# Unmasked attention by sorting and prefix sums instead of a full aggregation, in a four-layer graph attention kernel

## The chip, the cores and the metric

The kernel runs on one core of a Trainium2 chip. The metric is the device time of one execution in microseconds (us). Engines: TensorE (PE; its weight loads are PEld), VectorE (DVE), ScalarE (ACT), GpSimd (POOL) and SyncE (SP), which issues most DMAs. Each engine works through its own queue in order; semaphores tie the queues together.

## The reference

`x` has shape (32, 512, 256): 32 independent batches of 512 tokens with 256 features. Four layers follow each other, and all of them add to `x`. Each starts with a layer norm and a ReLU, and holds one or two graph attentions. An attention computes `h = inp @ W`, a score per pair of tokens from two numbers per token, and a softmax-weighted mean of the rows of `h`:

```python
def _gat(inp, adj_mask, W, a):
    h = jnp.matmul(inp, W)
    f1 = jnp.matmul(h, a[:F_, 0]); f2 = jnp.matmul(h, a[F_:, 0])
    e = jax.nn.leaky_relu(f1[:, :, None] + f2[:, None, :], ALPHA)
    if adj_mask is not None:
        e = jnp.where(adj_mask[None, :, :] > 0, e, NEG_INF)
    att = jax.nn.softmax(e, axis=2)
    h_prime = jnp.einsum('bij,bjf->bif', att, h)
    return jax.nn.elu(h_prime)
# layer 3
out = relu(x @ mlp1_w + mlp1_b);  residual = out            # 256 -> 512
out = elu(_gat(relu(out), None, W_fc, a_fc)) + residual     # no mask, 512 wide
out = relu(out @ mlp2_w + mlp2_b); residual = out           # 512 -> 256
out = relu(elu(_gat(relu(out), adj, W_hand, a_hand)) + residual)
```

Layers 0 and 1 have one masked attention of 256 features, layer 2 has four masked heads of 64, and layer 3 is the block above. Its first attention has no mask: every token sees all 512.

## The kernel before

All arithmetic is in float32. The 512 tokens are four tiles of 128 partitions (`NT = 4`). The attention weight exp(leaky_relu(r + t)) is written, after common factors are taken out, as the larger of a number of the row (`r`) and a number of the column (`t`), times a factor of the column that is multiplied into the values. So `weights` (L238 to L252) transposes `r` into a bank of PSUM by four TensorE transposes (L243), and VectorE takes the maximum with `t` and multiplies by the mask (L247; without a mask L251). `aggregate` (L257, matmuls at L259) multiplies the 512 x 512 weights with the values; a column of factors beside the values gives the denominator (L263 takes its reciprocal). The unmasked attention of layer 3 does this with 512 columns of values in two halves: 257 and 256 columns, four output tiles, four matmuls each.

The norm (`norm_t`, L177 on) takes statistics on VectorE (L182, L183), the reciprocal root on POOL (L185, L186), and writes `xn` on VectorE (L190). `xn` is transposed (L198), and ScalarE evicts it with the ReLU (L199). `linear_t` (L234, evicted at L235) and the value matmuls (L216, L317, L357) follow. `elu2_plus1` (L284 to L287) applies two ELUs with a min on VectorE, an Exp on ScalarE and an add on POOL.

Batches run in four streams (`NS = 4`); stream i takes batches i, i+4 and so on. Each layer is a Python generator that yields between steps, and a loop takes one step of each stream in turn:

```python
while live:
    for g in list(live):
        if next(g, live) is live:
            live.remove(g)
```

Before the next stream joins, the ones that are there take 20 rounds (`LEAD`). The order in which instructions are written is their priority; the scheduler of the framework, which simulates the engines, then fixes each engine's order when the kernel is built. Tiles come from pools with a number of buffers for each tag: eight banks of PSUM (`b`) for all streams, five weight tiles `w` of 8 KB a partition, three `v`, two `v2` and `v3`, eight `y`.

At the end the kernel computes a flag from the mask and from the largest exponential it has seen (`seen`, L208). If it is set, a general version of the kernel runs instead. With the given inputs it does not.

Of the kernel before, what the change touches and what calls it, by code (L numbers as in the profile page):

```python
# [21 lines left out]
I32 = mybir.dt.int32  # L22
AF = mybir.ActivationFunctionType
# [6 lines left out]
NEG = -(2.0 ** 100)  # L30


@with_exitstack
def fast(ctx, tc, flag, x, adj, w0, a0, w1, a1, w2, a2, mlp1_w, mlp1_b, mlp2_w, mlp2_b,
# [10 lines left out]
    LEAD = 20  # L45
# [3 lines left out]
    psum = ctx.enter_context(tc.tile_pool(name="psum", bufs=1, space=bass.MemoryType.PSUM))  # L49

    def bank():
        return psum.tile([P, N], FP, tag="b", name="b", bufs=8)
# [9 lines left out]
    def load_x(b):  # L62
        t = work.tile([P, NT, F], FP, tag="x", name="x", bufs=NS + 1)
        nc.sync.dma_start(t, x[b].rearrange("(t p) f -> p t f", p=P))
        return t
# [16 lines left out]
    def project(dst, block, kt, a_cols):  # L82

        ft, n = a_cols.shape[1], a_cols.shape[2]
        for k in range(kt):
            p = bank()
            for f in range(ft):
                nc.tensor.transpose(p[:, f * P:(f + 1) * P], block(k, f), ident)
            wT = work.tile([P, N], FP, tag="y", name="wT", bufs=8)
            nc.scalar.copy(wT[:, :ft * P], p[:, :ft * P])  # L90
            q = bank()
            for f in range(ft):
                nc.tensor.matmul(
                    q[:, :n], wT[:, f * P:(f + 1) * P], a_cols[:, f, :], start=(f == 0), stop=(f == ft - 1)
                )
# [22 lines left out]
    adj_sb = work.tile([P, NT, N], I32, tag="w", name="adj", bufs=5)  # L118
    nc.sync.dma_start(adj_sb, adj.rearrange("(t p) j -> p t j", p=P))
    pos = work.tile([P, NT, N], FP, tag="w", name="pos", bufs=5)  # L120
    nc.vector.tensor_scalar(pos, adj_sb, 0.0, None, op0=OP.is_gt)
    own = work.tile([P, NT, N], FP, tag="w", name="own", bufs=5)
# [5 lines left out]
    for j in range(NT):  # L128
        p = bank()
        for t in range(NT):  # L130
            nc.tensor.transpose(p[:, t * P:(t + 1) * P], own[:, t, j * P:(j + 1) * P], ident)
# [8 lines left out]

    W1 = load_w(w1, a1, 0.01, "W1")
    CH = D + 3
    W2 = const.tile([P, KF, NH, CH], FP, name="W2")
    raw2 = work.tile([P, KF, F], FP, tag="y2", name="raw2", bufs=4)
# [32 lines left out]
    def norm_t(xt):  # L177
# [9 lines left out]
        yield  # L187
        xn = work.tile([P, NT, F], FP, tag="xn", name="xn", bufs=3)
        for t in range(NT):
            nc.vector.tensor_scalar(  # L190
                xn[:, t, :], xt[:, t, :], mv[:, t, 0:1], rs[:, t:t + 1], op0=OP.subtract, op1=OP.mult
            )
        yield
        hT = work.tile([P, KF, N], FP, tag="hT", name="hT", bufs=3)
        for k in range(KF):
            p = bank()
            for t in range(NT):
                nc.tensor.transpose(p[:, t * P:(t + 1) * P], xn[:, t, k * P:(k + 1) * P], ident)  # L198
            nc.scalar.activation(hT[:, k, :], p, AF.Relu)  # L199
        yield  # L200
# [9 lines left out]
    def values(hT, w):  # L210

        v = work.tile([P, NT, F + 3], FP, tag="v", name="v", bufs=3)
        for t in range(NT):
            ps = bank()
            for k in range(KF):
                nc.tensor.matmul(  # L216
# [5 lines left out]
            if t % 2:  # L222
                yield
# [3 lines left out]
    def linear_t(inT, w, bias, name):  # L227
# [3 lines left out]
        for f in range(ft):  # L231
            p = bank()
            for k in range(kt):
                nc.tensor.matmul(p, w[:, k, f * P:(f + 1) * P], inT[:, k, :], start=(k == 0), stop=(k == kt - 1))  # L234
            nc.scalar.activation(o[:, f, :], p, AF.Relu, bias=bias[:, f:f + 1])  # L235
            yield
        return o

    def weights(r_col, t_col, masked=True):

        r = bank()
        for t in range(NT):
            nc.tensor.transpose(r[:, t * P:(t + 1) * P], r_col(t).to_broadcast([P, P]), ident)  # L243
        wt = work.tile([P, NT, N], FP, tag="w", name="w", bufs=5)
# [9 lines left out]
    def pair():  # L254
        return work.tile([P, 2, F], FP, tag="y", name="y", bufs=8)

    def aggregate(p, wt, t, rhs):  # L257
        for j in range(NT):
            nc.tensor.matmul(p, wt[:, j, t * P:(t + 1) * P], rhs(j), start=(j == 0), stop=(j == NT - 1))  # L259
# [6 lines left out]
    def plain(hT, w):  # L266
        v = yield from values(hT, w)
        wt = weights(lambda t: v[:, t, F + 2:F + 3], lambda j: v[:, j, F + 1:F + 2])
        yield
# [19 lines left out]
    def layer0(xt):  # L289
        v, wt = yield from plain((yield from norm_t(xt)), W0)  # L290
        for t0 in range(0, NT, 2):
            r, q = pair(), pair()
            for i in range(2):
                p, rd = averages(v, wt, t0 + i)
                nc.scalar.activation(q[:, i, :], p, AF.Exp, scale=rd)  # L295
                nc.scalar.activation(r[:, i, :], p, AF.Relu, scale=rd)
            add_elu(xt[:, t0:t0 + 2, :], r, q)
            yield

    def layer1(xt):  # L300
        v, wt = yield from plain((yield from norm_t(xt)), W1)
        for t0 in range(0, NT, 2):
            r = pair()
            for i in range(2):
                p, rd = averages(v, wt, t0 + i)
                nc.scalar.activation(r[:, i, :], p, AF.Relu, scale=rd)
            xr = xt[:, t0:t0 + 2, :]
            nc.gpsimd.tensor_tensor(xr, xr, r, op=OP.add)  # L308
            yield

    def layer2(xt):
        hT = yield from norm_t(xt)
        v = work.tile([P, NT, NH, CH], FP, tag="v2", name="v2", bufs=2)
        for t in range(NT):
            ps = bank()
            for k in range(KF):
                nc.tensor.matmul(  # L317
# [7 lines left out]
            if t % 2:  # L325
                yield
        note(v.rearrange("p t h c -> p (t h) c")[:, :, D:])
        ys = [pair(), pair()]
        for h in range(NH):
            wt = weights(lambda t: v[:, t, h, D + 2:D + 3], lambda j: v[:, j, h, D + 1:D + 2])  # L330
            yield
# [5 lines left out]
            for i in range(2):  # L337
# [548 lines left out]
```

## Time and profile before

| | |
|---|---|
| median of 3 runs | 3417.73 us (3411.73 to 3418.64) |
| profiled execution, its own time | 3417.93 us |
| its span, first to last instruction | 3416.2 us |
| granted TensorE clock, mean | 0.977 |
| busy: PE, PEld, DVE, ACT, POOL | 3314.6, 2750.0, 1700.9, 1380.6, 571.7 us |
| HBM read, written | 20.99, 16.78 MB |

A row of a group of instructions reads: line, engine, operation, output <- inputs, shapes, count, then busy time in us and mean ns of one, then the idle time of the engine just before them and what ended it. A float32 matmul leaves two records in the trace, a transpose one. Matmuls overlap at their ends, so the busy times of groups add up to more than the engine's busy time. In the waits, the first name is who waited and the second is what came last. The granted clock is the share of full speed that TensorE was given.

### The profile page before, as it was taken

The numbers are of one execution on the slowest core, as the hardware profiler recorded it, in microseconds if no ns is written. First come the engines' busy times: TensorE is split into PE (matmuls) and PEld (weight loads), VectorE is DVE, ScalarE is ACT, GpSimd is POOL, SyncE is SP. The second block draws the span as 40 slices with busy tenths as digits, with TensorE's granted clock in tenths as the row PEclk, the third lists the DMA queues.
The fourth block names the chain that finished last, engine by engine and source line by source line (L and its number), as shares of the span: only waits on it lengthen the run. The fifth ranks groups of instructions, "written<-read, shape, count | busy, mean of one in ns | idle before, by whom it ended". The sixth has DMA issues, their size and how long they took to land.

```text
span 3416.2 us, 44221 instructions
## 1 busy us (share of the span) xinstructions
PE 3314.6 (97%) x17265; PEld 2750.0 (80%) x17265; DVE 1700.9 (50%) x4422; ACT 1380.6 (40%) x3281; POOL 571.7 (17%) x583
## 2 busy tenths in 40 slices
PE   6899999999999999999999999999999999999997
PEld 5688888788887887878878888788888788887875
DVE  3554563554644655446544455454653545635542
ACT  2234434444334434344334443444434444344433
POOL 0111111211112111121111121112201111112111
PEclk8899999999999999999999999999999999999999
DMA  2000000000000000000000000000000000000000
GB/s 80 1 1 13 13 1 13 13 13 13 1 13 13 13 13 1 13 19 7 13 13 1 25 7 7 13 1 25 13 1 13 11 16 13 1 13 7 7 7 14
DMA packets 41606, 40.67 MB, mean 12 GB/s; under 512 B 5296, under 2 KB 40624, under 8 KB 41392
## 3 DMA queue, kind: packets, MB, share of 16 engines
q1 hardware_dynamic: 41392, 37.77, 3.6%
q8 instruction: 140, 2.29, 0.3%
q14 instruction: 74, 0.61, 0.1%
HBM read 20.99 MB, written 16.78 MB: 11 GB/s over the span
## 4 chain that ended last, share of the span: by engine, by line
PE 87%; DVE 6%; ACT 3%; POOL 3%; issue 1%; DMA 0%; SPq 0%; POOLq 0%; ACTq 0%; DVEq 0%
PE b L259 43%; PE b L357 13%; PE b L234 11%; PE b L216 8%; PE b L317 3%; PE b L198 3%; PE b L243 3%; PE b L387 1%; DVE xn L190 1%; POOL y L287 1%; DVE st L182 1%; DVE x L281 1%; POOL rs L186 1%; PE b L405 1%; DVE y L280 1%
## 5 line engine op out<-in xcount | busy, mean ns | idle before, releaser
L259 PE MATMUL b<-v,w 128*128 128x257 f32 (+2 forms) x9216 | 1657.9, 337 | 19.2 <-DVE w L247 16.9
L259 PEld LDWEIGHTS b<-v,w 128*128 128x128 f32 x9216 | 1457.2, 194 | 218.5 <-issue 44.0
L247 DVE SCALAR_TENSOR_TENSOR w<-b,v,maskT 128x512 f32<-128x512 f32 x896 | 609.2, 744 | 37.3 <-PE b L243 37.3
L287 POOL TENSOR_TENSOR y<-y 128x512 f32<-128x512 f32 x192 | 243.4, 1268 | 1799.2 <-ACT y L286 1566.7
L263 DVE RECIPROCAL rden<-b 128x1 f32<-128x1 f32 (+1 forms) x640 | 101.9, 166 | 756.2 <-PE b L259 755.4
L357 PE MATMUL b<-WFC,oT 128*128 128x259 f32 (+1 forms) x2048 | 466.4, 380 | 0.0
L357 PEld LDWEIGHTS b<-WFC,oT 128*128 128x128 f32 x2048 | 381.9, 189 | 62.5 <-issue 8.1
L190 DVE TENSOR_SCALAR xn<-x,mv,rs 128x256 f32<-128x256 f32 x512 | 190.8, 432 | 153.1 <-POOL rs L186 153.1
L216 PE MATMUL b<-W,hT 128*128 128x259 f32 x1024 | 263.4, 402 | 2.1 <-ACT hT L199 2.0
L182 DVE BATCH_NORM_STATS2 st<-x 128x6 f32<-128x256 f32 x512 | 194.4, 406 | 98.3 <-POOL x L308 67.1
L234 PE MATMUL b<-hT,WM 128*128 128x512 f32 x512 | 240.8, 593 | 0.0
L234 PE MATMUL b<-oT,WM 128*128 128x512 f32 x512 | 232.2, 596 | 0.5 <-DVE oT L390 0.5
L216 PEld LDWEIGHTS b<-W,hT 128*128 128x128 f32 x1024 | 195.4, 200 | 34.2 <-ACT hT L199 7.3
L295 ACT ACTIVATE y<-b,rden 128x256 f32<-128x256 f32 x128 | 60.8, 475 | 395.6 <-DVE rden L263 395.6
L379 ACT ACTIVATE y<-b,rden 128x256 f32<-128x256 f32 x256 | 123.2, 481 | 222.7 <-DVE rden L263 173.1
L199 ACT ACTIVATE hT<-b 128x512 f32<-128x512 f32 x256 | 142.3, 595 | 143.7 <-PE b L198 142.5
L221 ACT ACTIVATE v<-b,v 128x256 f32<-128x256 f32 x384 | 182.5, 475 | 12.5
L234 PEld LDWEIGHTS b<-oT,WM 128*128 128x128 f32 x512 | 95.8, 191 | 95.4 <-issue 87.5
L285 DVE TENSOR_SCALAR y<-y 128x512 f32<-128x512 f32 x192 | 82.4, 429 | 178.5 <-ACT y L379 142.4
L364 ACT ACTIVATE v<-b,v 128x256 f32<-128x256 f32 x256 | 121.5, 475 | 117.8 <-PE b L357 113.6
L198 PE MATMUL b<-ident,xn 128*128 128x128 f32 x1024 | 145.0, 283 | 19.1 <-DVE xn L190 19.1
L286 ACT ACTIVATE y<-y,minus 128x512 f32<-128x512 f32 x192 | 138.8, 723 | 57.3 <-DVE y L285 41.4
(99 smaller groups left out, 2892.8 us busy)
## 6 DMA issues: line engine op xcount, KB each, us to landing
x<-in_x_dram SPq DMA_DIRECT2D x32, 512.0 KB, 3.8
out_dram<-x SPq DMA_DIRECT2D x32, 512.0 KB, 2.9
adj<-in_adj_dram SPq DMA_DIRECT2D x1, 1024.0 KB, 8.1
WM<-in_L_gnn_mlp_w_dram SPq DMA_DIRECT2D x2, 512.0 KB, 5.4
WFC<-in_L_gnn_W_fc_dram SPq DMA_DIRECT2D x2, 512.0 KB, 5.7
W<-in_L_gnn_W_dram SPq DMA_DIRECT2D x2, 256.0 KB, 7.8
raw<-in_L_gnn_W_dram SPq DMA_DIRECT2D x1, 256.0 KB, 5.6
WHA<-in_L_gnn_W_hand_dram SPq DMA_DIRECT2D x1, 256.0 KB, 6.2
```

The lines of the kernel that those rows point to most:

```text
L182: nc.vector.bn_stats(st[:, t, :], xt[:, t, :])
L190: nc.vector.tensor_scalar(xn[:, t, :], xt[:, t, :], mv[:, t, 0:1], rs[:, t:t + 1], op0=OP.subtract, op1=OP.mult)
L198: nc.tensor.transpose(p[:, t * P:(t + 1) * P], xn[:, t, k * P:(k + 1) * P], ident)
L199: nc.scalar.activation(hT[:, k, :], p, AF.Relu)
L216: nc.tensor.matmul(ps[:, :F + 3], hT[:, k, t * P:(t + 1) * P], w[:, k, :], start=(k == 0), stop=(k == KF - 1))
L221: nc.scalar.activation(v[:, t, :F], ps[:, :F], AF.Copy, scale=pj)
L234: nc.tensor.matmul(p, w[:, k, f * P:(f + 1) * P], inT[:, k, :], start=(k == 0), stop=(k == kt - 1))
L247: nc.vector.scalar_tensor_tensor(wt[:, j, :], r, t_col(j), maskT[:, j, :], op0=OP.max, op1=OP.mult)
L259: nc.tensor.matmul(p, wt[:, j, t * P:(t + 1) * P], rhs(j), start=(j == 0), stop=(j == NT - 1))
L286: nc.scalar.activation(q, q, AF.Exp, bias=minus1)
L287: nc.gpsimd.tensor_tensor(r, r, q, op=OP.add)
L357: nc.tensor.matmul(ps[c][:, :n], oT[:, k, t * P:(t + 1) * P], WFC[:, k, c * (F + 3):c * (F + 3) + n], start=(k == 0), stop=(k == KH - 1),)
```

## The change

1. **The unmasked attention.** For a row with number r, the tokens with t below r contribute r times their value, and the others t times their value. With the tokens sorted by t, the sum of any row is therefore r times a prefix sum of the values plus a suffix sum of t times the values, both read at the place where r falls. The changed kernel no longer builds the 512 x 512 weights there. It transposes `t` (`tj`), finds each token's rank by comparing with all others on VectorE (ties broken by the token's index, `tie`), and finds the place of each r by a sum of signs on ScalarE. Four indirect DMAs from POOL scatter the rows of `v3` to DRAM (`order`) in sorted order. SP reads them back in two halves of 258 columns, four consecutive sorted rows a partition. POOL and VectorE add the four rows up inside the partition, two matmuls with triangular matrices (`before`, `after`) carry the sums across partitions, and SP writes the 513 rows of prefix and suffix sums to DRAM (`table`). Four indirect DMAs gather one row of the table for each token, and VectorE, ScalarE and POOL finish as before.
2. **The norm.** `xn` is written by ScalarE, with scale and bias and the ReLU, from two more small POOL operations. The eviction of the transposes is a plain copy.
3. **Streams.** Each stream has a clock; the stream with the earliest clock takes the next step. The clock advances by the time of the step's TensorE columns times 2.4 and by the number that the step yields. Streams start 80 apart.
4. **Buffers.** Every stream has two PSUM banks and one `x` tile of its own. `w` has four buffers, `v` and `v2` share four, `v3` has one, `y` and `q` three each; layer 2 writes one tile `y4`.

The core of the diff (`matmul` and `transpose` count columns and call TensorE):

```diff
     def bank():
-        return psum.tile([P, N], FP, tag="b", name="b", bufs=8)
+        return psum.tile([P, N], FP, tag=f"b{turn[0]}", name="b", bufs=8 // NS)
...
+        mr = small([NT], "mr")
+        nc.gpsimd.tensor_tensor(mr, mv[:, :, 0], rs, op=OP.mult)
+        nc.gpsimd.tensor_scalar_mul(mr, mr, -1.0)
+        yield 4
+        xn = work.tile([P, NT, F], FP, tag="xn", name="xn", bufs=2)
         for t in range(NT):
-            nc.vector.tensor_scalar(
-                xn[:, t, :], xt[:, t, :], mv[:, t, 0:1], rs[:, t:t + 1], op0=OP.subtract, op1=OP.mult
-            )
+            nc.scalar.activation(xn[:, t, :], xt[:, t, :], AF.Relu, bias=mr[:, t:t + 1], scale=rs[:, t:t + 1])
...
         note(v[:, :, F:F + 3])
-        wt = weights(lambda t: v[:, t, F + 2:F + 3], lambda j: v[:, j, F + 1:F + 2], masked=False)
-        yield
-        for t in range(NT):
-            y, q = pair(), pair()
-            for c, n in ((0, F + 1), (1, F)):
-                ps = bank()
-                aggregate(ps[:, :n], wt, t, lambda j: v[:, j, c * (F + 3):c * (F + 3) + n])
-                if c == 0:
-                    rd = reciprocal(ps[:, F:F + 1])
-                nc.scalar.activation(q[:, c, :], ps[:, :F], AF.Exp, scale=rd)
-                nc.scalar.activation(y[:, c, :], ps[:, :F], AF.Relu, scale=rd)
-            elu2_plus1(y, q)
+        tj = work.tile([P, N], FP, tag="tj", name="tj", bufs=1)
+        p = bank()
+        for t in range(NT):
+            transpose(p[:, t * P:(t + 1) * P], v[:, t, F + 1:F + 2].to_broadcast([P, P]), ident)
+        nc.scalar.copy(tj, p)
+        yield 1
+        found = small([2, NT], "found")
+        for t in range(NT):
+            nc.vector.scalar_tensor_tensor(
+                junk, tj, v[:, t, F + 1:F + 2], tie(t), op0=OP.subtract, op1=OP.is_lt,
+                accum_out=found[:, 0, t:t + 1],
+            )
+            nc.scalar.activation(
+                junk, tj, AF.Sign, bias=v[:, t, F + 2:F + 3], scale=-1.0, accum_out=found[:, 1, t:t + 1]
+            )
+        at = work.tile([P, 2, NT], U32, tag="at", name="at", bufs=4)
...
+        order = dram.tile([N, H + 3], FP, tag="order", name="order", bufs=2)
+        for t in range(NT):
+            nc.gpsimd.indirect_dma_start(
+                out=order, out_offset=bass.IndirectOffsetOnAxis(ap=at[:, 0, t:t + 1], axis=0),
+                in_=v[:, t, :], in_offset=None,
+            )
+        yield 18
+        for c in range(2):
+            flat = work.tile([P, NT * 2, C], FP, tag="sums", name="sums", bufs=2)
+            sums = flat.rearrange("p (t k) n -> p t k n", k=2)
+            u = sums[:, :, 1, :]
+            nc.sync.dma_start(u, rows[:, :, c * (F + 1):c * (F + 1) + C])
...
+            nc.gpsimd.tensor_tensor(sums[:, 2, 0, :], u[:, 0, :], u[:, 1, :], op=OP.add)
+            nc.gpsimd.tensor_tensor(sums[:, 3, 0, :], sums[:, 2, 0, :], u[:, 2, :], op=OP.add)
+            nc.gpsimd.tensor_tensor(tot, sums[:, 3, 0, :], u[:, 3, :], op=OP.add)
+            nc.vector.tensor_scalar_mul(u[:, 3, :], u[:, 3, :], T[:, 3:4])
+            for t in (2, 1, 0):
+                nc.vector.scalar_tensor_tensor(
+                    u[:, t, :], u[:, t, :], T[:, t:t + 1], u[:, t + 1, :], op0=OP.mult, op1=OP.add
+                )
+            yield 5
+            pv, pu = bank(), bank()
+            matmul(pv[:, :C], before, tot, start=True, stop=True)
+            matmul(pu[:, :C], after, u[:, 0, :], start=True, stop=True)
+            nc.scalar.copy(sums[:, 0, 0, :], pv[:, :C])
+            nc.vector.tensor_tensor(
+                sums[:, 1:, 0, :], sums[:, 1:, 0, :], pv[:, None, :C].to_broadcast([P, NT - 1, C]), op=OP.add
+            )
+            nc.vector.tensor_tensor(u, u, pu[:, None, :C].to_broadcast([P, NT, C]), op=OP.add)
...
+            nc.sync.dma_start(places[:, :, c, :], flat)
+            nc.sync.dma_start(table[N:, c * C:(c + 1) * C], tot[P - 1:, :])
+            yield 10 * c
+        for t in range(NT):
+            y, q = pair(), pair("q")
+            g = work.tile([P, 4 * C], FP, tag="g", name="g", bufs=3)
+            nc.gpsimd.indirect_dma_start(
+                out=g, out_offset=None, in_=table,
+                in_offset=bass.IndirectOffsetOnAxis(ap=at[:, 1, t:t + 1], axis=0),
+            )
+            z = g[:, :2 * C]
+            nc.vector.scalar_tensor_tensor(z, z, rr[:, t:t + 1], g[:, 2 * C:], op0=OP.mult, op1=OP.add)
+            rd = reciprocal(z[:, F:F + 1])
+            nc.scalar.activation(q, z, AF.Exp, scale=rd)
+            nc.scalar.activation(y, z, AF.Relu, scale=rd)
+            elu2_plus1(y, q)
+            yield 6
+            p = bank()
+            for f in range(KH):
+                transpose(p[:, f * P:(f + 1) * P], y.rearrange("p a f -> p (a f)")[:, f * P:(f + 1) * P], ident)
...
+    live = {i: i * LEAD for i in range(NS)}
+    streams = [stream(i) for i in range(NS)]
     while live:
-        for g in list(live):
-            if next(g, live) is live:
-                live.remove(g)
+        i = min(live, key=live.get)
+        turn[0], spent[0] = i, 0.0
+        wait = next(streams[i], None)
+        if wait is None:
+            del live[i]
+        else:
+            live[i] += STRETCH * spent[0] / CYCLES + wait
```

## The prediction

> **What bounds the kernel now.** I read the page's busy times first, then busy time by windows, the chain of waits, the groups with shapes kept apart, and the DMA issues. From the page (busy us, share of the span, instructions; the chain by engine):
>
> ```profile
> PE 3314.6 (97%) x17265; PEld 2750.0 (80%) x17265; DVE 1700.9 (50%) x4422; ACT 1380.6 (40%) x3281; POOL 571.7 (17%) x583
> ...
> PE 87%; DVE 6%; ACT 3%; POOL 3%; issue 1%; DMA 0%; SPq 0%; POOLq 0%; ACTq 0%; DVEq 0%
> ```
>
> TensorE sets the end; nobody else is above 50%. The windows (busy time of PE, PEld, DVE, ACT, POOL, then the granted clock) show that this holds all through:
>
> ```profile
> 440.88:853.94 413.06, 408.33 (x2145) 339.81 (x2145) 210.94 (x549) 170.98 (x408) 71.14 (x72) 0.99 0.03 11
> ```
>
> 413.06 us is one round of four batches, 103.3 a batch, and PE idles 1% of it. What the change takes off PE therefore comes off the end one for one, until a new wait fills the hole. The outer stretches are different:
>
> ```profile
> 120.00:130.00 10.00, 10.00 (x39) 8.48 (x39) 4.04 (x10) 1.68 (x4) 0.00 (x0) 0.75 0.00 0
> 130.00:140.00 10.00, 5.16 (x38) 4.52 (x37) 7.02 (x22) 3.76 (x8) 1.26 (x2) 0.77 0.01 2
> 3300.00:3320.00 20.00, 18.71 (x124) 15.33 (x122) 10.01 (x22) 5.38 (x11) 2.53 (x2) 1.00 0.01 1
> ```
>
> Near the start, where PE has idled, the granted clock is 0.75 even in a window that is 100% busy: 2.5 us of 10 are lost. A PE gap can cost more than its own length.
>
> **PE work removed and added.** The chain in order of time gives PE time without overlaps (start, us, what):
>
> ```profile
> 3363.15 14.13 PE b L259 x64
> ```
>
> These 64 records (a float32 matmul leaves two) are the unmasked aggregation of one batch: 32 matmuls, 0.442 us each. All 32 batches: 452.2 us, gone. Added are four 128x258 triangular matmuls a batch, 128 in all, at the same 0.442: 56.6. The transposes keep their number (four for `tj` instead of four for `r`; 16 of `y`). Net -395.6 us, 12.4 a batch. PE's steady need is then 91 us a batch.
>
> **The other engines.** By the groups (busy, mean ns):
>
> ```profile
> L190 DVE TENSOR_SCALAR xn<-x,mv,rs 128x256 f32<-128x256 f32 x512 | 190.8, 432 | 153.1 <-POOL rs L186 153.1
> L221 ACT ACTIVATE v<-b,v 128x256 f32<-128x256 f32 x384 | 182.5, 475 | 12.5
> L186 POOL TENSOR_TENSOR rs<-rs,neg_half 128x4 f32<-128x4 f32 x128 | 135.0, 1060 | 6.7
> L251 DVE TENSOR_SCALAR w<-b,v 128x512 f32<-128x512 f32 x128 | 90.9, 746 | 17.3 <-PE b L243 17.3
> L287 POOL TENSOR_TENSOR y<-y 128x512 f32<-128x512 f32 x192 | 243.4, 1268 | 1799.2 <-ACT y L286 1566.7
> ```
>
> DVE loses the norm's 190.8, the 90.9 of L251 and 8 in layer 2. It gains 128 searches like L247 (0.744): 95; 256 products of 258 columns at L190's 0.432: 111; per half a 774-, a 1032- and a small 258-column add from PSUM, at L390's 684 ns for 512 scaled up about 0.95 + 1.22 + 0.42, times 64: 166; 128 combinations at L280's 0.70: 90; small copies 26. DVE: about 1900 us. ACT gains 512 norms at L221's 0.475 (243), 128 Signs at 0.72 (92), copies (80), and saves 85 where 512 reads of a half row become 256 of a whole row: about 1710. POOL gains 256 four-element operations at L185's 0.226 (58) and 192 adds of 258 columns (1.268 x 258/512 = 0.64: 123), and the making of 256 indirect DMAs: bounds per issue are 0.23 (L185) and 1.06 (L186, whose ucode also loops), I take the middle 0.64: 164. About 920. Against a span near 3200 these are 59%, 53% and 29%: covered by PE, at no cost, as long as no PE instruction waits for their queues. If that cover went, DVE's extra 200 us is the most it could show.
>
> **The new waits, which decide.** Layer 3 now leaves the chip twice. Engines run their queues in order, so the question is how much PE work the built order puts between the steps. I priced the changed kernel's PE order with the rows above (group sums scaled by 0.927, since the groups of before add up to 3575 us against 3314.6 busy). The same four distances repeat each round, one per stream:
> - last `tj` transpose to first `before` matmul: 21.6, 24.8, 21.8, 23.6; mean 22.9 us
> - last `after` matmul to the first `y` transpose: 16.3, 17.2, 16.3, 11.3; mean 15.3 us
>
> Against the first stands: copy of `tj` 0.60 (L199); the stretch of DVE's queue from the first search to the index copy, 5.3 to 7.3, mean 6.2; four scatters, each waiting for the landing of the one before (all write `order`), 4S; the read of half the rows, 516 KB; three POOL adds 1.9. DMA rows (KB each, us to landing):
>
> ```profile
> x<-in_x_dram SPq DMA_DIRECT2D x32, 512.0 KB, 3.8
> out_dram<-x SPq DMA_DIRECT2D x32, 512.0 KB, 2.9
> adj<-in_adj_dram SPq DMA_DIRECT2D x1, 1024.0 KB, 8.1
> A<-in_L_gnn_a_dram SPq DMA_DIRECT2D x8, 0.2 KB, 2.5
> ```
>
> The read is 3.8, so the need is 12.5 + 4S. The trace has no DMA from POOL and none that is indirect. S is bounded by 2.5, the quickest landing, and 8.1, the slowest; a gain is excluded, the old kernel had no such step. The nearest row is the 2.9 store; with 0.64 to make it, S = 3.5. Need 26.5 against 22.9: PE waits 3.6 us a batch.
>
> The Trainium skill, DMA: Bandwidth & Descriptors, section Anatomy of one DMA, fits a POOL-issued DMA as 2.0 us plus bytes/436e3: 2.6 us for a scatter of 258 KB, as an estimate. No run here shows it yet; by it the first wait would vanish and the end would be near 3075. SBUF — State Buffer, section Who interferes with whom, speaks against the change: DVE in its fast two-port mode locks GpSimd out, and descriptors wait; its example goes from 0.62 to 3.1 us. If each scatter met that, an estimate of S would be 6.0 and of the end 3590, slower; no row here shows it.
>
> Against the second distance: DVE add 1.22; write of a table half, 1032 KB, between 2.9 and twice that, I take 4.4; gather 3.8 + 0.64; combination 0.70, reciprocal 0.16, Exp 0.63, min 0.43, Exp 0.72, POOL add 1.27. Sum 13.9 against 15.3: only the stream with 11.3 waits, 2.6, so 0.65 on average.
>
> While scatters two to four wait, POOL's queue stands 3S = 10.5 us a batch, and behind them are other streams' norm (L232 to L236) and residual adds (L336, L359, L532). POOL's free share covers the sum; the delay lies inside the wait already counted. SP's queue holds row reads, table writes, loads of `x` and stores in order; none feeds PE sooner than two batches' time apart except this chain, so I add nothing.
>
> Gaps of 4 us or more lower the clock: 2.5 us each by the window at 120, taken for half the batches: 1.25. Two banks per stream instead of eight shared: between 0 and 3% of PE; I take 0, since the built order puts other streams between a stream's banks, and keep 90 us for the range. `v3` and `tj` have one buffer; the next batch's first L357 comes 27 to 70 us after `tj`, past the scatters, so 0. The common clock's order has no price of its own: its spacing is in the distances, and if it mixes the streams worse than the old rounds, that shows as the same 0 to 90 us before ordinary matmuls. At the end the last two batches have no neighbours to hide in (the last has 13 and 2 us of PE work in the two distances): about 30 us more than now.
>
> **Sum**, against the profiled execution's own 3417.93 (span 3416.2; the median of the runs shown is 3417.73, so it stands for them): 3417.9 - 395.6 + 30 + 32 x (3.6 + 0.65 + 1.25 = 5.5, 176) = 3228 us.
>
> **Rivals.**
> - *All waits covered.* If S is 2.5, the first need is 22.5, below 22.9; only 0.65 stays: 3417.9 - 395.6 + 30 + 21 = 3073. For it: the 1% idle of the steady round shows how well four streams fill PE. Against: the landing of 2.9 is the best for a store. 18%.
> - *Slower: the scatter chain takes PE's place.* Break-even is a loss of 365.6/32 = 11.4 a batch. Less 2.5 of clock and 0.65, 8.25 must come from the first wait: 4S = 18.65, S = 4.7. At 5.6 (the median landing of the 512 KB weight loads) the wait is 12, the loss 15.2 a batch: 3417.9 - 365.6 + 485 = 3537. For it: four landings in a row on one queue, made in software, beside DVE at 59%. Against: HBM is idle (12 GB/s). 20%.
> - *The change does nothing here*: the flag sends the run into the general code as well. The limit on `seen` and the mask test are untouched, so under 1%; it would add far more than any range.
>
> **How the numbers follow.** The forecast's case (faster, waits of 1 to 11 us a batch) has 60%, the covered one 18%, slower 20%, within 0.2% (7 us, about what a measurement of this kernel can tell from no change) 2%. The range starts below the covered case at 3060 and ends at S = 5: (9.6 + 0.65 + 2.5) x 32 = 408, 3460. Some 6% lie below, 14% above.
>
> **What would show it.** PE busy near 2920. A group at the triangular matmuls with idle before it, put down to POOL adds or the row read, some 115 us in all; another at the `y` transposes. Scatter landings of 3 to 4 us. Granted clock still above 0.95. I am wrong if scatters land after 4.7 or more, if the idle stands before ordinary matmuls on ACT (banks) or the norm's transposes on POOL, or if DVE or ACT is on most of the chain.

## The result and the profile after

The changed kernel takes 3589.10 us (median of 4, 3583.14 to 3596.40) against 3417.66 for the kernel before: a ratio of 1.0506, 95% interval 1.0482 to 1.0531. It is 171 us slower where 190 us less was forecast. The profiled execution took 3583.14 us, its span is 3581.4 and its mean granted clock 0.937.

Page after (busy us, share of the span, instructions):

```profile
PE 3113.2 (87%) x15473; PEld 2442.9 (68%) x15473; DVE 1963.6 (55%) x4651; ACT 1697.4 (47%) x3953; POOL 1046.9 (29%) x1290
```

PE's instructions are down by 1792: the 2048 records of the removed aggregation, less 256 of the triangular matmuls. The work went as the diff says. But PE now idles 468 us (span less busy), before it was 102. Busy time by windows of the kernel after, columns as before (PE, PEld, DVE, ACT, POOL, granted clock), again one round of four batches:

```profile
1506.85:1939.24 432.39, 379.79 (x1921) 298.91 (x1920) 242.13 (x577) 210.41 (x492) 130.78 (x161) 0.95 0.21 69
```

A batch takes 108.1 us instead of 103.3, and PE is idle in 12% of the round instead of 1%. It runs at 0.95 instead of 0.99. In this round no other engine is above 57%, so nobody took PE's place as the bound: PE waits. For whom, says the view of PE's waits (us in total, times, longest):

```profile
PE b L65 <- ACT xn L240: 148.6, 94, 7.9
PE b L65 <- POOL y L336: 121.7, 43, 16.6
PE b L61 <- POOL tot L465: 57.5, 34, 3.9
...
PE b L61 <- DVE w L296: 20.2, 32, 3.0
```

In the kernel before, the three largest are:

```profile
PE b L387 <- POOL y L287: 23.8, 24, 2.5
PE b L198 <- DVE xn L190: 19.1, 5, 6.1
PE b L259 <- DVE w L247: 16.9, 34, 1.0
```

After the change, the matmuls and transposes stand at the helpers' lines L61 and L65. The largest wait is at the transposes of the norm (`xn`), which the sort does not touch. The second is at the transposes of the gathered rows (`y`), and only the third at the triangular matmuls (`tot`), where the forecast had put most of it. The groups and DMA rows that answer to the priced ones (busy us, mean ns; KB, us to landing):

```profile
L240 ACT ACTIVATE xn<-x,mr,rs 128x256 f32<-128x256 f32 x512 | 275.8, 592 | 251.8 <-POOL mr L236 251.8
L444 POOL DMA_INDIRECT order<-v,at x128 | 135.8, 1061 | 735.0 <-DVE at L438 385.8 <-DVE mv L230 173.2 <-DMA order<-v,at 112.4
L494 DVE SCALAR_TENSOR_TENSOR g<-g,rr 128x516 f32<-128x516 f32 x128 | 136.9, 1069 | 129.6 <-DMA g<-table,at 128.6
...
table<-sums SPq DMA_DIRECT2D x64, 1032.0 KB, 5.3
sums<-order SPq DMA_DIRECT2D x64, 516.0 KB, 5.9
order<-v,at POOLq DMA_INDIRECT x128, 2.9
g<-table,at POOLq DMA_INDIRECT x128, 5.1
```

One batch's way to the triangular matmul, from the timeline (start, us, engine, what, idle before it):

```profile
1692.10 0.59 ACT L423 COPY tj<-b 128x512 f32<-128x512 f32 x1
1701.26 1.12 POOL L444 DMA_INDIRECT order<-v,at  x1 [30.19 <-DVE at L438]
1705.90 1.14 POOL L444 DMA_INDIRECT order<-v,at  x1 [3.52 <-issue]
1709.60 0.96 POOL L444 DMA_INDIRECT order<-v,at  x1 [2.56 <-DMA order<-v,at]
1713.16 1.09 POOL L444 DMA_INDIRECT order<-v,at  x1 [0.57 <-issue]
1713.28 1.68 PE L65 MATMUL b<-ident,xn 128*128 128x128 f32 x6 [6.02 <-ACT xn L240]
1716.09 1.25 SPq L457 DMA_DIRECT2D sums<-order  x2
1722.55 0.70 PE L61 MATMUL b<-tot,before 128*128 128x258 f32 x2 [0.71 <-POOL tot L465]
```

From the copy of `tj` to the matmul it is 30.5 us, 26.5 were forecast. Over all 32 batches it is 24.8 to 31.8 us, with a mean of 28.4. The scatters stand 4.64, 3.70 and 3.56 us apart here; over all 96 pairs the mean is 3.59 (forecast: 3.5). PE waits for the triangular matmul for 0.71 us only. So the part of the forecast that was worked out most carefully is nearly right, and most of the loss is elsewhere: in the same stretch PE stands 6.02 us before the norm of another stream.

### The profile page after: what moved, and what is told of

Same layout as the page of the kernel before. It is cut to its first block, busy times and chain, and to the rows that moved or that the text cites. A ratio compares the mean times of both kernels' runs of the same rounds, so it can differ in the third digit from the quotient of the medians.

```text
span 3581.4 us, 43201 instructions
## 1 busy us (share of the span) xinstructions
PE 3113.2 (87%) x15473; PEld 2442.9 (68%) x15473; DVE 1963.6 (55%) x4651; ACT 1697.4 (47%) x3953; POOL 1046.9 (29%) x1290
## 5 line engine op out<-in xcount | busy, mean ns | idle before, releaser
L61 PE MATMUL b<-v,w 128*128 128x65 f32 (+1 forms) x7168 | 1269.8, 329 | 53.1 <-ACT y L356 25.6
L61 PEld LDWEIGHTS b<-v,w 128*128 128x128 f32 x7168 | 1097.4, 198 | 185.4 <-ACT y L356 31.3
L61 PE MATMUL b<-WFC,oT 128*128 128x259 f32 (+1 forms) x2048 | 506.0, 391 | 0.1
L336 POOL TENSOR_TENSOR y<-y,q 128x512 f32<-128x512 f32 x192 | 251.8, 1311 | 664.9 <-ACT q L335 423.0
L61 PEld LDWEIGHTS b<-WFC,oT 128*128 128x128 f32 x2048 | 385.6, 196 | 54.3 <-issue 3.3
L61 PE MATMUL b<-W,hT 128*128 128x259 f32 (+1 forms) x1536 | 396.2, 392 | 3.0 <-ACT hT L247 2.6
L240 ACT ACTIVATE xn<-x,mr,rs 128x256 f32<-128x256 f32 x512 | 275.8, 592 | 251.8 <-POOL mr L236 251.8
L65 PE MATMUL b<-ident,xn 128*128 128x128 f32 x1024 | 211.4, 327 | 150.1 <-ACT xn L240 148.6
L61 PEld LDWEIGHTS b<-W,hT 128*128 128x128 f32 x1536 | 276.1, 192 | 71.7 <-ACT hT L247 22.1
L65 PEld LDWEIGHTS b<-ident,xn 128*128 128x128 f32 x1024 | 140.5, 165 | 230.2 <-ACT xn L240 201.0
L61 PE MATMUL b<-hT,WM 128*128 128x512 f32 x512 | 267.2, 648 | 6.5 <-ACT hT L247 6.5
L61 PE MATMUL b<-oT,WM 128*128 128x512 f32 x512 | 235.0, 603 | 1.6 <-DVE oT L507 1.6
L489 POOL DMA_INDIRECT g<-table,at x128 | 136.0, 1063 | 291.0 <-DMA table<-sums 192.6
L494 DVE SCALAR_TENSOR_TENSOR g<-g,rr 128x516 f32<-128x516 f32 x128 | 136.9, 1069 | 129.6 <-DMA g<-table,at 128.6
L65 PE MATMUL b<-ident,y 128*128 128x128 f32 x512 | 97.0, 315 | 121.8 <-POOL y L336 121.7
L247 ACT COPY hT<-b 128x512 f32<-128x512 f32 x256 | 138.6, 591 | 100.3 <-PE b L65 100.0
L335 ACT ACTIVATE q<-q,minus 128x512 f32<-128x512 f32 x192 | 138.5, 721 | 85.4 <-DVE q L334 83.3
```

The source lines that it names most:

```text
L61: nc.tensor.matmul(p, w, x, **flags)
L65: nc.tensor.transpose(p, x, i)
L240: nc.scalar.activation(xn[:, t, :], xt[:, t, :], AF.Relu, bias=mr[:, t:t + 1], scale=rs[:, t:t + 1])
L247: nc.scalar.copy(hT[:, k, :], p)
L335: nc.scalar.activation(q, q, AF.Exp, bias=minus1)
L336: nc.gpsimd.tensor_tensor(r, r, q, op=OP.add)
```

## The experiments

Times are compared with the kernel before as measured beside them (3411 to 3419 us). Where no interval is given, it is one execution. The framework fixes the order of each engine's queue anew for every kernel, so each edit below also moves some instructions; a difference of 10 or 20 us between two kernels need not come from the edit's own effect.

**1. Is it POOL's queue?** Here the scatters stand in POOL's queue ahead of a norm. Timeline after, the longest idle of PE in that stretch:

```profile
1516.06 1.26 POOL L359 TENSOR_TENSOR x<-x,y 128x512 f32<-128x512 f32 x1
1517.48 0.99 POOL L444 DMA_INDIRECT order<-v,at  x1 [0.16 <-issue]
1518.54 0.23 POOL L232 TENSOR_SCALAR rs<-mv 128x4 f32<-128x4 f32 x1
1518.85 1.04 POOL L233 TENSOR_TENSOR rs<-rs,neg_half 128x4 f32<-128x4 f32 x1
...
1520.53 0.60 ACT L240 ACTIVATE xn<-x,mr,rs 128x256 f32<-128x256 f32 x1 [4.80 <-POOL mr L236]
...
1521.18 0.69 PE L65 MATMUL b<-ident,xn 128*128 128x128 f32 x2 [3.86 <-ACT xn L240]
```

The residual add and a scatter come before the norm's root, ScalarE stands 4.80 us with everything that is queued behind it, and PE 3.86 us. Two kernels take the norm out of this queue, in whole or in part. The first computes root and bias on VectorE (a first guess from the bits of the number, then two Newton steps), the second writes `xn` on VectorE as before:

```diff
-        nc.gpsimd.tensor_tensor(rs, rs, neg_half, OP.pow)
...
+        nc.vector.tensor_scalar(rs.bitcast(I32), ri, -1.0, float(0x5F375A00), op0=OP.mult, op1=OP.add)
...
+            nc.vector.scalar_tensor_tensor(rs, sq, 1.5, rs, op0=OP.add, op1=OP.mult)
...
-        nc.gpsimd.tensor_tensor(mr, mv[:, :, 0], rs, op=OP.mult)
+        nc.vector.scalar_tensor_tensor(mr, mv[:, :, 0], -1.0, rs, op0=OP.mult, op1=OP.mult)
```

> Changed kernel, but the reciprocal root of the norm and the bias are worked out on VectorE (a first guess from the bits, two Newton steps, ten small operations), so that no norm passes POOL's queue. Theory A (POOL's queue is in order; while it stands at a scatter or gather, the norms of other streams stand behind it): TensorE's waits for xn (148.6 us) fall below 40, the granted clock rises from 0.937 to 0.95 or more, time 3380 to 3480 us. Theory B (the DRAM round trips are longer than the PE work between their steps, POOL's queue matters little): the waits move to the y and tot transposes, time 3540 to 3620 us, since VectorE gets 200 us more. Theory C (two banks a stream and the common clock's order cost the time): same as B.

```diff
-            nc.scalar.activation(xn[:, t, :], xt[:, t, :], AF.Relu, bias=mr[:, t:t + 1], scale=rs[:, t:t + 1])
+            nc.vector.tensor_scalar(
+                xn[:, t, :], xt[:, t, :], mv[:, t, 0:1], rs[:, t:t + 1], op0=OP.subtract, op1=OP.mult
+            )
```

> Changed kernel with the norm of before: xn written by VectorE, ReLU at the eviction, two POOL operations instead of four. Theory A (in-order POOL queue): the root is still behind the DMAs on POOL, so the waits for xn stay above 90 us and the time at 3530 to 3600 us. Rival (the norm waits because its chain got longer: 592 ns on ScalarE against 432 ns, and two more POOL steps): waits for xn below 50 us, time 3420 to 3500 us.

Measured: 3580.5 and 3565.8 us, 9 and 23 less than the changed kernel's median, whose own executions lie 13 apart. POOL's busy time fell from 1047 to 803 us in the first, and PE still waits 117 us before the norm's transposes in both, while the waits for `w` on VectorE grew from 20 to 56 and 60. POOL's queue is one link; with it gone, the next one is late: with ten small VectorE operations, the way from a norm's statistics to its last `xn` got longer, 7.6 us on average in the first against 6.1 in the changed kernel. The changed kernel's trace says the same of POOL. In the example above, the root begins 2.4 us after the last statistics, but over all 128 norms the mean is 1.06 us, and in the kernel before it is 0.91. So the norm's place in POOL's queue is not the main cause of the loss. The adds of the ELU and of the residual stayed on POOL in both kernels and are not tested by them.

**2. The frame without the sort.** The changed kernel, with the full aggregation put back in layer 3: clock, norm on ScalarE, banks and buffers of the change. Its layer 3 yields 3 once where the sort yields 18 and more, so the streams' clocks run differently there.

> Changed kernel without the sorting: the unmasked attention is the full aggregation again, while the norm on ScalarE, the streams' clocks and the buffers of the change stay. PE gets its 12.4 us a batch back. Theories A and B: with no DMA on POOL the steady rounds idle 1 to 3%, time 3420 to 3480 us. Theory C: the frame itself idles, 8 us a batch or more remain, time 3600 us or more.

Measured: 3584.5 us (median of 4), ratio 1.0488 (1.0471 to 1.0506). The page's PE line:

```profile
PE 3358.2 (94%) x17265; PEld 2726.7 (76%) x17265; DVE 1528.4 (43%) x3787; ACT 1596.0 (45%) x3793; POOL 630.7 (18%) x842
```

This is the run that turns the case. The frame alone costs 167 us: PE has the same 17265 instructions as before, idles 226 us instead of 102, and is busy 44 us longer with them at the same granted clock of 0.977; no run here shows why. And in this frame the sort, which takes away 1792 instructions, moves the time by under 5 us: PE's busy time falls by 245 us, and its idle time grows by 243.

**3. Which part of the frame?** Five kernels. With eight banks shared by all streams:

```diff
-        return psum.tile([P, N], FP, tag=f"b{turn[0]}", name="b", bufs=8 // NS)
+        return psum.tile([P, N], FP, tag="b", name="b", bufs=8)
```

> The full aggregation in the new frame (e3, 3584.5 us), with the eight PSUM banks shared by all streams again. Theory C1 (two banks a stream make PE wait for evictions and break its order into small pieces): most of the 167 us over the kernel before goes, 3420 to 3480 us. Theory C2 (the common clock puts too little PE work between the end of a layer and the next norm's transposes) and C3 (fewer y, q, w, xn and v buffers): 3550 to 3600 us, and the waits for xn stay near 66 us.

3608.4 us: the banks by themselves are not it. With the steps taken in rounds again (31 rounds before the next stream joins), at the change's finer steps:

```diff
-        i = min(live, key=live.get)
...
+        for e in list(live):
+            turn[0] = e[0]
+            if next(e[1], live) is live:
+                live.remove(e)
```

> The full aggregation in the new frame (e3), but the streams take one step each in turn as before (31 rounds before the next stream joins, the share of a batch that the 20 of before were), with two banks a stream and all other buffers of the change. Theory C2: the waits for xn fall from 66 us to below 20, time 3430 to 3500 us. Theory C1 or C3: 3560 us or more, the idle stands before matmuls that wait for an eviction or for a buffer.

3797.0 us: with these fine steps, rounds are worse still. With more buffers than the change has (5 `w` for 4, 2 `v3` for 1, 3 `xn` for 2, 5 `v` for 4, 5 `y` and 5 `q` for 3):

> The full aggregation in the new frame (e3, 3584.5 us) with room again: five w, two v3, three xn, five v, five each of y and q; clock, two banks a stream and the norm on ScalarE stay. Theory C3 (the cut buffers are what costs the 167 us): 3420 to 3470 us. Theory C2 (the common clock's order): 3560 us or more.

3555.5 us, 29 less. The same with eight shared banks (the diff above) and the norm on VectorE (the second diff of part 1), which is close to the kernel before with finer steps taken by the clock:

> As h1, and with eight shared banks and the norm on VectorE with POOL's root as before: what is left of the change is the common clock with its finer steps. Theory C2: 3540 to 3620 us. Theory C3: 3410 to 3450 us.

3560.6 us, 142 above before. Last, the kernel before with its own coarse steps, and only the choice of the next stream changed (the streams start 80 apart):

```diff
-        for g in list(live):
-            if next(g, live) is live:
-                live.remove(g)
+        i = min(live, key=live.get)
+        spent[0] = 0.0
+        if next(streams[i], live) is live:
+            del live[i]
+        else:
+            live[i] += 2.4 * spent[0] / 2400.0 + 3.2
```

> The kernel before, its coarse steps and its work unchanged; only who goes next is decided by the common clock (each step costs 3.2 plus 2.4 times its matmul columns at full clock, the streams start 80 apart). If the finer steps are what cost 142 us, this stays within 30 us of 3418. If the clock by itself costs them (it puts other batches' steps between those of one batch than rounds do), 3500 to 3600 us.

3589.7 us, 173 above before. So it is the clock, at least as it is tuned here, and not the finer steps. PE's waits in this run:

```profile
PE b L55 <- DVE w L257: 71.9, 96, 1.6
PE b L59 <- DVE xn L200: 68.8, 18, 6.1
```

In the kernel before, those for `w` sum to 16.9 us and those for `xn` to 19.1. This reads as if the clock left less of other streams' work between a step and its use on PE than the rounds did; the distances were not counted.

**4. The norm alone, and the buffers alone,** in the kernel before. The norm first (part 2 of the change and nothing else: the reverse of the second diff of part 1, with the two POOL operations for `mr`):

> The kernel before with the norm of the change alone: xn by ScalarE, two more POOL operations, plain copy at the eviction. Theories C2 and C3 both: within 20 us of the kernel before. A fourth theory, the longer norm chain (2.4 + 0.4 us more from the statistics to the last xn) is what makes PE wait: 3440 to 3520 us.

3517.4 us, 99 above before. The group of the norm, from its page:

```profile
L193 ACT ACTIVATE xn<-x,mr,rs 128x256 f32<-128x256 f32 x512 | 283.1, 600 | 225.1 <-POOL mr L189 225.1
```

ScalarE stands 225 us in front of these for POOL's root. In the kernel before it was VectorE that stood there (153 us, L190 in the prediction). ScalarE evicts the banks that PE's next matmuls read, and these wait behind the norm: PE's waits for `v` on ScalarE are 55 us in this run.

The buffers:

```diff
-        wt = work.tile([P, NT, N], FP, tag="w", name="w", bufs=5)
+        wt = work.tile([P, NT, N], FP, tag="w", name="w", bufs=4)
...
-        xn = work.tile([P, NT, F], FP, tag="xn", name="xn", bufs=3)
+        xn = work.tile([P, NT, F], FP, tag="xn", name="xn", bufs=2)
...
-        v = work.tile([P, NT, H + 3], FP, tag="v3", name="v3", bufs=2)
+        v = work.tile([P, NT, H + 3], FP, tag="v3", name="v3", bufs=1)
```

> The kernel before (rounds, eight shared banks, norm on VectorE) with one v3 instead of two, four w instead of five, two xn instead of three. Theory C3: 3500 to 3600 us. Theory C2: 3415 to 3440 us.

3402.6 us, and measured again (below) 3403.69 us. Fewer of these three buffers cost nothing in the order of before.

**5. The sort's own waits,** in the changed kernel. With two buffers for `tot` in place of one:

```diff
-            tot = work.tile([P, C], FP, tag="tot", name="tot", bufs=1)
+            tot = work.tile([P, C], FP, tag="tot", name="tot", bufs=2)
```

> Changed kernel with two buffers for tot instead of one, so that the second half's total need not wait until the first half's row has landed in the table (36 us of POOL waiting, 14 times, some 4 us in each of those batches). Theory B (length of the DRAM chain): the wait before the first triangular matmul of the second half goes, time 3530 to 3570 us. Theory A alone: the same wait holds POOL's queue, so a similar gain; no change at all (within 10 us) would say that the first triangular matmul is late for the scatters, not for tot.

3540.8 us, 48 less: the one buffer was held by the small store of the table's last row (36 us of POOL's waits were for it). The next kernels start from this one. With wider spacing of the steps that yield a length and, separately, with eight shared banks:

```diff
-            live[i] += STRETCH * spent[0] / CYCLES + wait          # STRETCH = 2.4
+            live[i] += STRETCH * spent[0] / CYCLES + 1.5 * wait    # STRETCH = 1.6
```

> The changed kernel with two tot buffers (e4, 3540.8 us) and every yielded number times 1.5, the factor on PE columns 1.6 instead of 2.4, so that a batch takes about as long on the streams' clock, but more of it lies behind the steps that wait for other engines or DMAs. Theory C2, and theory B for the sort: waits for xn, y and tot (130.7, 104.8, 27.2 us) fall to a half or less and the granted clock rises above 0.95; 3300 to 3430 us. Theory C1: two banks with closer matmuls of one stream wait more for evictions; 3540 us or more.

> The changed kernel with two tot buffers (e4, 3540.8 us) and eight shared banks. Theory C1: 3350 to 3430 us, as much gained as f1 gains on e3. Theories B and C2: 3500 to 3560 us, waits for xn and y stay above 90 us.

3600.4 and 3801.8 us. Spacing is not simply too short: the waits for `xn` fall from 131 to 75 us, but those for `tot` rise from 27 to 53, and others come. With shared banks, idle at `tot` rises to 181 us and the clock falls to 0.898, perhaps because one stream's late step holds banks that the others need. The change's banks for each stream are right for the sort in this order. Then what is read back no longer waits for DRAM. All instructions are still issued, but the sums are of ones, so these two kernels do not compute the attention:

```diff
-        rows = order.rearrange("(p t) c -> p t c", t=NT)
+        rows = rows0        # m1 and m2: written once at the start
...
-                out=g, out_offset=None, in_=table,
+                out=g, out_offset=None, in_=table0,    # m2 only
```

> The changed kernel with two tot buffers (3540.8 us), in which the sorted rows are read from a buffer written once at the start: the scatters still go out, but nothing waits for them. Output differs: the prefix sums are of ones. Theory T (the trips through DRAM are what PE waits for): the waits on tot (27 us) and part of those on y (105 us) go, and the clock rises: 3400 to 3490 us. Rival O (the waits come from the order of the queues and of the norms, not from the trips): within 40 us of 3541.

> As m1, and the gathers read a table written once at the start, so they do not wait for the table's write either; every instruction of the sort still goes out, only the waits through DRAM are gone (output differs: every gathered row is ones). Theory T: the waits on y go too and the clock comes near the 0.977 of the dense kernel in this frame; 3250 to 3380 us. Rival O: 3480 to 3560 us.

3471.0 and 3495.7 us. Without the wait for the scatters the kernel is 70 us faster; without that for the table it gains nothing that one run can show (the second was 25 slower). PE's waits in the first of them:

```profile
PE b L65 <- ACT xn L247: 127.9, 77, 7.9
PE b L65 <- POOL y L343: 112.4, 28, 10.4
```

The waits for `tot` are gone, those for `xn` and `y` stay, and PE still idles 407 us. In the second, the waits for `y` fall to 77 us and those for `xn` rise to 180. So the first lies in theory T's range, and the second in that of rival O. Neither kernel takes out all that the trips do. The scatters still wait for one another, and POOL's queue stands for that (115 us in the first, 112 in the changed kernel). The built order moved as well: about a sixth of POOL's instructions have another place in its queue.

**6. The sort in the order of before.** Rounds, coarse steps, eight banks, norm on VectorE; three yields after the scatters, one before the triangular matmuls, two before the gathers, one for each gathered tile. The second has 8 `y` for 6 and 4 `x` for 5; the two further steps that its expectation names are not in the kernel, whose yields are those of the first:

```diff
-        yield 18
+        yield
+        yield
+        yield
```

> The sort alone, in the order of before: steps taken in rounds as before, 8 shared banks, the norm on VectorE; 1 v3, 4 w and 2 xn buffers, two tot buffers, both halves of the sorted rows read together. The order written out leaves about 19 to 26 us of PE work between the scatters' step and the triangular matmuls, and about 7 to 14 between these and the first gathered rows. Theory F (the change lost its time in the new frame: order and norm): the sort keeps most of its 396 us of PE work here, and pays a first wait of up to 4 us and a second of up to 8 a batch: 3418 - 396 + 32 x (4 to 12) = 3150 to 3400 us. Rival W (the sort's own waits and the lower clock eat the gain in any order): no better than 3418, and as much as 3560; idle near 12 us a batch or more on PE.

> The same with 8 y buffers in place of 6 and 4 x in place of 5, and with one more step of other batches before the triangular matmuls and one more before the gathers go out. Theory F: some 0 to 3 us a batch less waiting than without it, so 0 to 100 us faster than the kernel beside it. Rival W: within 40 us of it.

4144.6 and 4245.2 us, far outside both theories. PE's waits in the first:

```profile
PE b L488 <- POOL y L319: 285.0, 89, 18.6
PE b L458 <- POOL tot L448: 147.6, 18, 25.1
```

PE idles 807 us and its clock is 0.837. In this order and with these buffers the sort takes 604 us more than in the changed kernel with two `tot`. But the two differ in more than the choice of the next stream. The banks are shared here, and shared banks alone cost the sort 261 us under the clocks (part 5). The steps are coarse, and the norm is on VectorE. A likely reading is that rounds give each step the same share of other work, so that one step cannot get 25 us of cover without all the others. The sort in rounds with two banks for each stream, or with more yields at these places, was not run, so it is not shown that the sort needs the clocks.

**7. A version that beats both.** The kernel before with 1 `v3`, 4 `w` and 2 `xn` buffers:

> The kernel before with 1 v3, 4 w and 2 xn buffers, in five rounds against the kernel before. If the 16 us of the first look are real, the ratio is 0.994 to 0.997 with its interval below 1; if they are noise, 1.000.

3403.69 us (median of 8), ratio 0.9975 (0.9964 to 0.9985). It is the fastest kernel of this case, by a quarter of a per cent. Why fewer buffers help was not tried.

## Why the prediction was wrong

The sum was 3417.9 - 395.6 + 30 + 176 = 3228; the profiled execution took 3583. Term by term:

- *PE work, -395.6: nearly right in work, not in time.* Busy time times granted clock falls from 3281 (3358.2 x 0.977, the dense kernel in the same frame) to 2917 (3113.2 x 0.937): 364, where 395.6 x 0.977 = 386 was forecast. Against the kernel before it falls by 321 only, since the frame keeps PE busy longer with the same work. So PE busy, which was to be near 2920, is 3113: some 127 of these 193 us are the lower clock.
- *The order, banks and clock, priced at 0 with 90 for the range: the step that failed first.* The prediction says "The common clock's order has no price of its own: its spacing is in the distances". The distances were worked out for the two new steps only. In the other steps the spacing changed too, and that costs 173 us by itself in the kernel before. The whole frame costs 167, above the 90 that the range left for it.
- *The norm on ScalarE, priced at 0 because ScalarE is at 53%: failed.* Alone it costs 99 us. The condition was written down ("as long as no PE instruction waits for their queues") and not examined: the norm waits on POOL's root, and ScalarE's queue holds PE's evictions. The parts do not add (173 and 99 against 167 together), and inside the changed kernel the norm is worth 23 us at most.
- *First wait, 3.6 us a batch (115): too high by the waits.* PE's waits for `tot` are 57.5 us. Two `tot` buffers give 48 us and the cut wait for the scatters 70 more. That these add up to 118 is chance: the sum did not have the one `tot` buffer, and the 118 hold what the clock and the other waits gained. The spacing S was right (3.59); the read took 5.9 instead of 3.8.
- *Second wait, 0.65 a batch (21): failed.* PE waits 121.7 us for the gathered rows. Of this, 35.5 us stand in the last two batches, and the other 86 are 2.9 a batch. With the wait for the table cut too, no time is gained. The rows of the table's write (5.3, forecast 4.4), the gather (5.1, forecast 3.8 + 0.64) and the combination (1.07, forecast 0.70) are all above what was taken.
- *The end, 30 us: about right.* In the last 150 us PE idles 62 us, against 20 in the kernel before and 30 in the dense kernel in the new frame.
- *Clock, 1.25 a batch (40): too small.* Busy 3113.2 x (1 - 0.937/0.977) is 127 us more than at the clock of before. The clock record has half speed in 65 stretches, 453 us in all; in the kernel before it is 16 and 160. So there are 49 more such stretches where the sum had 16, and each takes about 3 us (half of 293 us over 49) where the sum had 2.5.
- *"Wrong if ... the idle stands before ... the norm's transposes on POOL": this is what is seen,* and the trace names POOL's `mr` as what ScalarE waited for. The first experiment shows that POOL's queue is still not the main cause.

The rival on the slower side gave 3537, close in time and wrong in cause: it needed scatters 4.7 us apart to break even and 5.6 for this time, and they are 3.59 apart on average. The prediction's other estimate on that side, 3590 us with scatters 6.0 apart, met the measured time by luck, for the same reason.

Where the 396 us went, then: about 118 to the trips and to `tot`, as far as kernels with a rebuilt order can tell. Without these the sort gains 114 us over the dense kernel in this frame (3584.5 to 3471.0). So 282 of 396 are missing even then: PE idles 407 us instead of 226 (182, mostly before `xn` and `y`), and 3062 busy us at a clock of 0.946 instead of 0.977 are about 97 more. That these come from the order of the queues, with less PE work a batch to hide the same chains of norm, ELU and residual, is argued: it fits what stays after both cuts, but no run here shows it alone, and the scatters' hold on POOL's queue stays in both.

The Trainium skill, DMA: Bandwidth & Descriptors, section Anatomy of one DMA, gave 2.6 us for a scatter as an estimate; the trace has a median of 2.9 from issue to landing, so it was near. SBUF — State Buffer, section Who interferes with whom, also says that a VectorE instruction with two SBUF inputs contends with a GpSimd instruction that reads SBUF, and that who issues first decides who blocks. The prediction used that section against the scatters; the trace shows contention of VectorE with POOL's adds (last section), and the scatters hardly further apart (3.59) than was forecast without it (3.5). On who blocks, the trace agrees in part: VectorE also lost where its record begins before that of the add, behind the making of a DMA (2.41 us in the rows below).

## What to carry over

Price a new order of the streams on every step, not on the steps that the change adds: a frame that moves all distances needs a run or a count of its own, and the cheapest one is the old work in the new frame. An engine at 50% is no cover for an instruction that waits for another engine, if PE's evictions are queued behind it. PE work that is taken out of a bound stage also takes away what hid the other chains; as far as these runs can tell, the gain ends where the next chain is no longer covered.

## What the runs showed of the hardware

The making of an indirect DMA holds POOL for 1.06 us, the upper end of what was allowed, and this is 272 us in the kernel.

VectorE's instructions with two inputs in SBUF and POOL's adds hold each other up. Timeline after, one batch's combinations (VectorE) and what POOL did:

```profile
1745.47 0.94 POOL L489 DMA_INDIRECT g<-table,at  x1 [0.30 <-issue]
1745.86 2.41 DVE L494 SCALAR_TENSOR_TENSOR g<-g,rr 128x516 f32<-128x516 f32 x1 [1.08 <-DMA g<-table,at]
1746.42 1.28 POOL L532 TENSOR_TENSOR x<-x,y 128x512 f32<-128x512 f32 x1
...
1748.51 0.76 DVE L494 SCALAR_TENSOR_TENSOR g<-g,rr 128x516 f32<-128x516 f32 x1
1748.93 1.47 POOL L359 TENSOR_TENSOR x<-x,y 128x512 f32<-128x512 f32 x1 [1.23 <-ACT y L356]
```

VectorE's instruction takes 2.41 us where it starts while POOL makes a DMA and then adds. Where VectorE is first, it takes 0.76, and POOL's add takes 1.47 in place of 1.28. It is the add that does it. Of the 128 combinations, 20 met the making of a DMA and no add after it, and they took 0.73 to 0.76 us. In 20 an add followed the making, and the mean is 1.85, the longest 3.70. In 20 an add was already running, and the mean is 1.38. The mean of all, 1.07 against 0.76, makes this some 40 us of VectorE.

A PE that idles in many places can be slow as well, but the share of idle time alone does not tell. The granted clock is 0.977 in the kernel before (3% idle) and still 0.977 in the dense kernel in the new frame (6%); it is 0.937 in the changed kernel (13%) and 0.837 in the sort in rounds (19%). PE's gaps of over 3 us sum to 34, 56, 225 and 548 us in these four, so in these four the clock is lower where the long gaps sum to more. In their clock records the clock is either full or half. From which length on a gap counts was not measured.
